# Output projection of token tiles in pairs by seven block products for eight

## The chip, the cores and the metric

The kernel runs on one core of one Trainium2 chip. Five engines work on it side by side: TensorE (PE) does matrix products into PSUM, VectorE (DVE), ScalarE (ACT) and GpSimd (POOL) do elementwise work, and SyncE (SP) issues the transfers (DMA). POOL works on SBUF tiles alone in this kernel. Each engine takes its instructions in order and waits on semaphores of the others. The metric is the device time of one execution in microseconds, the median of several runs.

## The reference

Everything is float32. `x` has 4 batches of 1024 tokens of 1024 features; there are 32 heads of 32 features.

```python
def attn(x, wq, wk, wv, wo):
    q, k, v = (x @ wq), (x @ wk), (x @ wv)          # each reshaped to (b, s, 32 heads, 32)
    q, k = rotary(q), rotary(k)
    scores = einsum('bqhd,bkhd->bhqk', q, k) / sqrt(32)
    probs = softmax(where(causal, scores, min))
    out = einsum('bhqk,bkhd->bqhd', probs, v).reshape(b, s, d)
    return out @ wo

def ffn(x, route_w, A, Bw):                          # 8 experts, rank 16, the best one alone
    logits = x @ route_w.T
    weight = one_hot(argmax(logits)) * max(logits)
    h = einsum('bsd,erd->bser', x, A)
    return einsum('bser,eor->bso', weight[..., None] * h, Bw)

x = x + attn(layernorm(x), wq, wk, wv, wo)
x = x + ffn(layernorm(x), route_w, A, Bw)
```

The change concerns `out @ wo` and the addition to `x` behind it.

## The kernel before

The work is cut into 32 units, one for each batch and each group of four heads (`units`; a batch has eight groups). A unit computes the scores of its heads in rounds (`score_round`, list `SLOTS`): PE fills four PSUM banks with the products of 32x32 blocks (L430), ACT copies them to SBUF (L441), POOL adds the causal mask on the diagonal (L444), DVE finds the row maxima (L462, and `both`, which joins the halves of a row, L483), ACT exponentiates (L491), and DVE transposes the probabilities in blocks of 32 (L516). Twice in a unit, at the slots "second" and "first", PE multiplies probabilities by values (`value_pieces`, L634) and DVE divides by the row sums (L654). A PSUM tile of four banks (`ps_s`) holds scores or values; four more banks (`ps`) serve everything else, one for each accumulation.

The probabilities of a unit lie in two tiles, `pr_{u}_0` and `pr_{u}_1` (tags `prob0`, `prob1`), each allocated anew for each unit. A query tile t takes a width that grows with t, and tiles stand `APART` from each other, so that between them there are places of at least 128 columns, in each of four heads, which hold nothing.

While a unit's scores, exponentials and values are computed, PE also works off a list of steps, `between[u]`, one list for each unit, which `fill` and `do_some` hand out slot by slot in proportion to their costs. A list holds the projections of the next unit (`chain`, L337: eight products for each of q, k, v and each half of the tokens, with the rotation behind q and k on DVE and POOL, L369 to L375), and, from the second batch on, the output projection of one token tile of the batch before (`finish_steps`).

That projection takes the attention values of 128 tokens, which each unit has stored to DRAM (`scratch`), back as `at`, transposed (`fetch`, which also loads the tile's `x` as `y`), and multiplies it by `wo` in two halves of 512 columns, eight products of 128x128 by 128x512 for each half (`project`, L751). A chunk of `wo` (256 KB) is loaded for each product into one of four buffers (`load_chunk`, L708), four ahead. DVE adds each half to `y` (L757), and behind the second half comes the layer norm (`layernorm`, L178 to L189: statistics, variance and the scaling on DVE, the root on POOL). The rest of a tile is its tail, four steps that stand in the list of the next unit: `turn` (eight transposes on PE, L201, copied back by ACT and DVE), `route` (L773, routing and hidden products, with five small operations on DVE), `turn_hidden` (L802) and `adapt` (L812, the adapters' product in two halves, each added to `y` by DVE, L815), and the store to `out`, SP's, a little later. So each of the eight units of a batch finishes one tile of the batch before; the last batch's tiles follow at the end, where `wo` is kept in SBUF.

The order of all instructions comes from this planner: steps are woven evenly (`weave`), rotations are put off by costs (`postponed`), and nothing reorders them afterwards. In the seventh unit of a batch that has a successor, the chains stand in the order `ENDING` and the last one is held back for the eighth, in which the layer norms of the next batch are woven in (`change_steps`, class `Norm`, whose `homes` say in which buffer a tile of `x` is put).

The row buffers (tag `row`, 128x1024) are five; a tile of the projection uses three of them, `at`, `y` and `yn`.

Of the kernel before, what the change touches and what calls it, by code (L numbers as in the profile page):

```python
# [9 lines left out]
F32 = mybir.dt.float32  # L10
# [61 lines left out]
def tile_preln_attn_then_top1_lora(  # L72
# [163 lines left out]
    class Two:  # L236
# [5 lines left out]
        def __getitem__(self, key):  # L242
            rows, cols = key
            k, at = divmod(cols.start, HALF)
            return self.parts[k][rows, at : at + cols.stop - cols.start]

    class Norm:


# [10 lines left out]
        def load(self, *tiles):  # L260
            u = self.b * NG
            for t in tiles:
                n = self.homes.get(t)
                if not n:
                    self.x[t] = load_x(self.b, t)
                    continue
# [421 lines left out]
    def load_adapter():  # L688

        ra_all = NC * (E + ER)  # L690
        room = big.tile([P, ra_all + D + TB * D], F32, tag="prob0", name="adapter")
# [25 lines left out]
    def finish_steps(b, t, kind="stream"):  # L717
# [126 lines left out]
        for c in range(0, NC, RA):  # L844
# [8 lines left out]
            Step(turn_hidden, 0.3),  # L853
            Step(adapt, 2.0, None if last else of_bw),
        ]
        return Step(fetch, 0.0), chains, tail


    def change_steps(u, norm, project, tail, held):
# [32 lines left out]
    tail = []  # L892
    for u, (b, g) in enumerate(units):
        project, new_tail = [], []
        if b:
            fetch, (project,), new_tail = finish_steps(
                b - 1, g, "resident" if u == len(units) - 1 else "stream"
            )
            if g:
                apart = 3 if g + 1 == NG and u + 1 < len(units) else 8  # L900
                between[-1].insert(max(0, len(between[-1]) - apart), fetch)
            else:
                late_fetch[u] = fetch

        if u + 1 < len(units) and g + 1 == NG:
            last_v = between[-1]
            if b:
                norm = Norm(b + 1, {0: (2,), 2: (5,), 3: (6,)}, {3: "q", 4: "k", 6: "q"})  # L910
                load = [Step(lambda norm=norm, t=t: norm.load(t), 0.0) for t in range(2)]
                for at, step in (
                    (own["k", 0][0], load[0]),
                    (own["v", 0][0], norm.finding(0)),
                    (own["v", 0][1], load[1]),
                    (own["v", 0][2], norm.scaling(0)),
                    (own["v", 0][4], norm.finding(1)),
                    (own["v", 0][6], norm.turning(0)),
                    (own["v", 0][7], norm.scaling(1)),
                    (own["k", 1][2], norm.finding(2)),  # L920
                    (own["k", 1][3], norm.turning(1)),
                    (own["k", 1][5], norm.scaling(2)),
                ):
                    behind(last_v, at, step)
            else:

                norm = Norm(b + 1, {0: (7,)}, {5: "chunk", 6: "chunk"})
                for v, t in (*((t + 1, t) for t in range(NG - 2)), (NG - 1, NT - 1)):
                    ahead_of[v] = (
                        lambda norm=norm, t=t: norm.find(t),  # L930
                        lambda norm=norm, t=t: norm.scale(t),
                    )
                    if v < NG - 1:
                        between[t].append(Step(lambda norm=norm, t=t: norm.load(t), 0.0))
                for at, step in (
                    (own["q", 0][0], Step(lambda norm=norm: norm.load(6), 0.0)),
                    (own["q", 1][0], norm.finding(6)),
                    (own["q", 1][3], norm.scaling(6)),
                ):
                    behind(last_v, at, step)  # L940
                for t, at in enumerate((("k", 1), ("k", 1), ("k", 1), ("v", 1))):
                    behind(last_v, own[at][(1 + 3 * t) % NC], norm.turning(t))
            steps = change_steps(u + 1, norm, project, tail, held)
            norms[b + 1] = norm
        else:
            steps = []
            held = []
            if u + 1 < len(units):


                ends = g + 2 == NG and b + 1 < B
                own = {}
                for n, tb in ENDING if ends else USUAL:
                    own[n, tb] = chain(u + 1, n, tb)
                    if ends and b and (n, tb) == ("v", 1):
                        held = own[n, tb]
                    else:
                        steps += own[n, tb]
            if not steps:
                steps = list(project)  # L960
            elif b and not g:
                steps = steps[:36] + weave(steps[36:], project)
            else:
# [263 lines left out]
```

## Time and profile before

| What | Value |
|---|---|
| Median of 3 runs | 2713.38 us (2710.95 to 2716.87) |
| Span of the profiled execution | 2709.0 us, the only time of its own that the page gives |
| PE busy | 2664.0 us, 98% |
| DVE, ACT, POOL busy | 2143.4 (79%), 1723.6 (64%), 601.9 us (22%) |
| Product of 128x128 by 128x512, L751 | 736 records with chunks, 602 ns each |
| Addition of a half to `y`, DVE L757 | 690 ns |
| POOL sum of two 128x512 tiles, L375 | 1289 ns |
| ACT copy of a 128x512 bank, L365 | 579 ns |
| 256 KB of `wo`, from issue to landing | 3.8 us |
| Mean granted TensorE clock | 0.998 |

A float32 product of the program leaves two records on PE; 368 loads of `wo` stand beside 736 records. Records overlap, so the distance of their starts, not their length, says what a product costs. In the timelines the columns are start, length, engine, line, operation, output and input with shapes, the number of records, and in brackets idle time and what ended it.

### The profile page before, as it was taken

How to read it: one execution, taken by the hardware profiler on the slowest of the kernel's cores; microseconds unless marked ns; L12 is line 12 of the kernel's file. 1: busy time of each engine (PE TensorE's matmuls, PEld its weight loads, DVE VectorE, ACT ScalarE, POOL GpSimd, SP SyncE). 2: the span in 40 equal slices, each digit the busy share in tenths (PEclk: the TensorE clock that was granted, in tenths of full speed). 3: DMA queues.
4: the chain of work that ended last, by engine and by line, in shares of the span. 5: the costliest groups of instructions: out<-in, count | busy, mean ns of one | idle time of the engine just before them, and what ended most of it. 6: DMA issues, size and time to landing. Idle time of an engine off the chain costs nothing.

```text
span 2709.0 us, 84062 instructions
## 1 busy us (share of the span) xinstructions
PE 2664.0 (98%) x35108; PEld 1300.3 (48%) x35108; DVE 2143.4 (79%) x4256; ACT 1723.6 (64%) x4978; POOL 601.9 (22%) x845
## 2 busy tenths in 40 slices
PE   8999999999999999999999999999999999999998
PEld 5444444444444544545444445444544444544445
DVE  4899988887787787887777877888787777787555
ACT  2878777876666676665666666766566666666521
POOL 2222222222222222222122222222212222212000
PEclk9999999999999999999999999999999999999999
DMA  3222323226554455652555554574355555446421
GB/s 119 60 72 73 76 72 80 64 65 176 139 141 130 124 138 154 165 164 65 164 158 134 136 132 131 137 189 140 83 158 143 154 134 138 122 132 198 127 70 53
DMA packets 465900, 332.74 MB, mean 123 GB/s; under 512 B 160880, under 2 KB 382320, under 8 KB 465520
## 3 DMA queue, kind: packets, MB, share of 16 engines
q1 hardware_dynamic: 465520, 327.37, 44.3%
q8 instruction: 276, 4.52, 0.7%
q14 instruction: 104, 0.85, 0.1%
HBM read 277.01 MB, written 50.26 MB: 121 GB/s over the span
## 4 chain that ended last, share of the span: by engine, by line
PE 80%; DVE 13%; ACT 3%; DMA 1%; issue 1%; POOL 1%; SPq 1%; POOLq 0%; DVEq 0%; ACTq 0%
PE po L751 15%; PE pq L337 14%; PE pk L337 14%; PE pv L337 12%; PE s L430 11%; PE av L634 8%; DVE top L462 4%; DVE pr L516 4%; PE ph L773 2%; PE pf L812 2%; ACT pr L491 1%; DVE both L483 1%; ACT pr L441 1%; PE pt_f L201 1%; DVE st_a L178 1%
## 5 line engine op out<-in xcount | busy, mean ns | idle before, releaser
L491 ACT ACTIVATE pr<-pr,both 128x256 f32<-128x256 f32 (+15 forms) x2048 | 1044.4, 518 | 53.6 <-DVE both L483 53.6
L441 ACT COPY pr<-s 128x640 f32<-128x640 f32 (+14 forms) x544 | 525.2, 1017 | 660.2 <-PE s L430 659.6
L462 DVE TENSOR_REDUCE top<-pr 128x2 f32<-128x960 f32 (+15 forms) x768 | 650.7, 894 | 251.4 <-POOL pr L444 250.8
L516 DVE STREAM_TRANSPOSE pr<-pr 128x1024 f32<-128x1024 f32 (+11 forms) x768 | 664.7, 908 | 34.1 <-ACT pr L491 30.7
L444 POOL TENSOR_TENSOR pr<-pr,causal_sb 128x128 f32<-128x128 f32 x512 | 237.2, 470 | 1158.3 <-ACT pr L441 1149.8
L337 PE MATMUL pv<-xnT,wv 128*128 128x512 f32 x1024 | 486.3, 602 | 0.0
L337 PE MATMUL pq<-xnT,wq 128*128 128x512 f32 x1008 | 478.1, 602 | 0.2 <-ACT xnT L203 0.2
L337 PE MATMUL pk<-xnT,wk 128*128 128x512 f32 x1008 | 477.1, 602 | 0.4 <-ACT rawq L363 0.4
L430 PE MATMUL s<-kT,qT 32*32 32x256 f32 (+4 forms) x17408 | 394.0, 386 | 9.4 <-POOL pr L444 3.2
L491 ACT ACTIVATION_READ_ACCUMULATOR pr<-pr,both 128x1 f32 x2048 | 400.8, 196 | 0.0
L751 PE MATMUL po<-chunk,attn 128*128 128x512 f32 x736 | 380.0, 602 | 2.5 <-DMA chunk<-in_wo 2.5
L430 PEld LDWEIGHTS s<-kT,qT 32*32 32x32 f32 x17408 | 187.3, 103 | 267.5 <-issue 100.7
L337 PEld LDWEIGHTS pk<-xnT,wk 128*128 128x128 f32 x1008 | 181.2, 190 | 235.7 <-issue 234.5
L337 PEld LDWEIGHTS pq<-xnT,wq 128*128 128x128 f32 x1008 | 183.2, 191 | 226.8 <-issue 225.0
L337 PEld LDWEIGHTS pv<-xnT,wv 128*128 128x128 f32 x1024 | 185.6, 190 | 218.1 <-issue 216.6
L634 PE MATMUL av<-pr,vals 64*32 64x256 f32 (+3 forms) x12288 | 272.8, 319 | 4.2 <-DVE pr L516 4.1
L634 PEld LDWEIGHTS av<-pr,vals 64*32 64x32 f32 x12288 | 213.0, 106 | 112.7 <-issue 66.1
L483 DVE TENSOR_TENSOR both<-top 32x4 f32<-32x4 f32 (+3 forms) x1152 | 207.4, 180 | 23.8
L751 PEld LDWEIGHTS po<-chunk,attn 128*128 128x128 f32 x736 | 135.6, 190 | 167.2 <-issue 149.4
L654 DVE TENSOR_TENSOR at<-av,by 128x256 f32<-128x256 f32 x128 | 48.2, 418 | 107.2 <-PE av L634 60.4
L751 PE MATMUL po<-wo,attn 128*128 128x512 f32 x256 | 116.6, 596 | 0.0
L375 POOL TENSOR_TENSOR qT<-qT,swapq 128x512 f32<-128x512 f32 x64 | 82.5, 1289 | 141.4 <-DVE swapq L371 141.4
(89 smaller groups left out, 1558.4 us busy)
## 6 DMA issues: line engine op xcount, KB each, us to landing
chunk<-in_wo SPq DMA_DIRECT2D x368, 256.0 KB, 3.8
vals<-vd SPq DMA_DIRECT2D x256, 128.0 KB, 4.3
x<-in_x SPq DMA_DIRECT2D x56, 512.0 KB, 5.4
wq<-in_wq SPq DMA_DIRECT2D x32, 512.0 KB, 4.7
wk<-in_wk SPq DMA_DIRECT2D x32, 512.0 KB, 4.0
wv<-in_wv SPq DMA_DIRECT2D x32, 512.0 KB, 4.3
vd<-vT SPq DMA_DIRECT2D x128, 128.0 KB, 4.6
out_y<-x SPq DMA_DIRECT2D x32, 512.0 KB, 2.6
```

The source lines that it names most:

```text
L337: nc.tensor.matmul(at["p"], lhsT=wt[:, c, :], rhs=xnTs[b, tb][:, c, :], start=(c == 0), stop=(c == NC - 1),)
L375: nc.gpsimd.tensor_tensor(dst[:, cols], dst[:, cols], other, ALU.add)
L430: nc.tensor.matmul(sc[i * SQ : (i + 1) * SQ, h, at : at + w].rearrange("p (j k) -> p j k", k=SQ), lhsT=of_q[rows, 2 * t + half], rhs=of_k[ ...
L441: nc.scalar.copy(pr[:, :, k0 : k0 + w], sc[:, :, at : at + w])
L444: nc.gpsimd.tensor_tensor(diagonal, diagonal, causal_sb.unsqueeze(1).to_broadcast([P, HG, SQ]), ALU.add)
L462: nc.vector.tensor_reduce(top[:, k, h : h + step], places[u, t][:, h : h + step, :], AX.X, ALU.max, negate=True,)
L483: nc.vector.tensor_tensor(dst[rows], src[rows], src[other], op)
L491: nc.scalar.activation(pr[:, h, :], pr[:, h, :], AF.Exp, bias=tops[u, t][:, h : h + 1], accum_out=dens[u, t // QT][:, t % QT, h : h + 1],)
L516: nc.vector.transpose(pr, pr)
L634: nc.tensor.matmul(avs[half][h * HD : (h + 1) * HD, t0:, :], lhsT=v[rows, j, h * HD : (h + 1) * HD], rhs=rhs, start=(j == 0), stop=(j == n ...
L751: nc.tensor.matmul(st["po"], lhsT=lhsT, rhs=rhs, start=(c == start), stop=(c == stop))
L773: nc.tensor.matmul(ph, lhsT=st["ynT"][:, c, :], rhs=w[:, c - i * RA, :], start=(c == 0), stop=(c == NC - 1),)
```

## The change

For tiles 1 and 2, 3 and 4, 5 and 6 of the first three batches, two token tiles are projected together (`pair_steps`). The two tiles' attention values and `wo` are each cut into 2x2 blocks, and the product of these is built from seven block products, p1 to p7, in place of eight. A block product is four PE products of 128x128 by 128x512, so a pair takes 28 in place of 32. Some products take sums of blocks:

- Four sums of blocks of `wo` are computed once, in the lists of the first four units, by four POOL subtractions in each, and kept in DRAM (`sum_wo`, `two_wo`): 16 loads and 16 stores of 256 KB.
- Four sums of attention blocks are computed by POOL for each pair, two of them into `s1` and `s2`, two in place.
- Products that go into more than one place are collected in `u2` and `u4`: ACT copies p1 to `u2`, DVE adds p6 to it, and p5 and that to `u4`; POOL adds `u2` and `u4` to `y` four times, and DVE adds p2, p3, p7 (twice) and p4 from PSUM.

`s1`, `s2`, `u2` and `u4` lie in the unused places between probability tiles (`gap`). For that the two probability tiles become fixed ones (`probs`). The gaps also take tile 1 of `x` of the third and fourth batch (class `Gaps`), in two transfers.

A pair's products stand in two lists: 14 in the odd unit (groups 1, 3, 5) and 14 in the even one. The first tile is complete behind p3 in the even unit, and its tail stands in the same list (`late_tail`), six or seven steps behind; the second tile's tail stands in the next unit's list, as before. The normalised tile replaces the attention values in their buffer, and the `x` tiles are loaded by steps of their own.

```diff
+    class Gaps(Two):
...
+                if n == "gap":
+                    self.x[t] = Gaps([gap(4), gap(5)])
+                    for k, part in enumerate(self.x[t].parts):
+                        source = x[self.b, t * P : (t + 1) * P, k * HALF : (k + 1) * HALF]
+                        nc.sync.dma_start(part, source.rearrange("p (c k) -> p c k", k=P))
...
+    probs = [big.tile([P, HG, WIDTH[k]], F32, tag=f"prob{k}", name=f"pr_{k}") for k in range(2)]
+    def gap(n):
+        blk, t = divmod(n, 3)
+        at = t * APART[blk] + (blk * QT + t + 1) * SQ
+        return probs[blk][:, :, at : at + P]
...
-            blocks[u, blk] = big.tile([P, HG, WIDTH[blk]], F32, tag=f"prob{blk}", name=f"pr_{u}_{blk}")
+            blocks[u, blk] = probs[blk]
...
+    two_wo = dram.tile([4, D // 2, 512], F32, tag="wo_sums", name="wo_sums", bufs=1)
+    def sum_wo(c):
+        rows = {}
+        def load():
+            for k in range(4):
+                i, n = divmod(k, 2)
+                wt = big.tile([P, 512], F32, tag="chunk", name=f"ws_{k}_{c}", bufs=4)
+                at = i * D // 2 + c * P
+                nc.sync.dma_start(wt, wo[at : at + P, n * 512 : (n + 1) * 512])
+                rows[i, n] = wt
+        def first():
+            nc.gpsimd.tensor_tensor(rows[0, 0], rows[0, 1], rows[0, 0], ALU.subtract)
+            nc.gpsimd.tensor_tensor(rows[0, 1], rows[1, 1], rows[0, 1], ALU.subtract)
+        def second():
+            nc.gpsimd.tensor_tensor(rows[1, 1], rows[1, 1], rows[0, 0], ALU.subtract)
+            nc.gpsimd.tensor_tensor(rows[1, 0], rows[1, 0], rows[1, 1], ALU.subtract)
+        def store():
+            for k, at in enumerate(((0, 0), (1, 1), (0, 1), (1, 0))):
+                nc.sync.dma_start(two_wo[k, c * P : (c + 1) * P], rows[at])
+        return [Step(f, 0.0) for f in (load, first, second, store)]
+    def pair_steps(b, t, t2):
+        st, tail = finish_steps(b, t, "pair")
+        st2, tail2 = finish_steps(b, t2, "pair")
+        s1, s2, u2, u4 = (gap(k) for k in range(4))
+        def fetch():
+            for k, tk in enumerate((t, t2)):
+                at = row(f"attn_{b}_{tk}").rearrange("p (c k) -> p c k", k=P)
+                nc.sync.dma_start(
+                    at, scratch[b][:, tk * P : (tk + 1) * P].rearrange("(c p) k -> p c k", p=P)
+                )
+                a[k, 0], a[k, 1] = at[:, : NC // 2], at[:, NC // 2 :]
+                (st, st2)[k]["home"] = at
...
+        def part(product, c, k):
...
+            if c == 0:
+                bank_of[product] = bank([P, 4, P], f"p{product}_{name}")
+            po = bank_of[product]
+            nc.tensor.matmul(
+                po.rearrange("p c k -> p (c k)"),
+                lhsT=lhsT()[:, c, :],
+                rhs=take_chunk(k),
+                start=c == 0,
+                stop=c == 3,
+            )
+            load_chunk(k + 4)
+            behind_product.get((product, c), lambda po: None)(po)
+        def sums_1(po):
+            nc.gpsimd.tensor_tensor(s1, a[1, 0], a[1, 1], ALU.add)
+        def sums_2(po):
+            minus(s2, s1, a[0, 0])
+        def sums_3(po):
+            minus(a[1, 0], a[0, 0], a[1, 0])
+        def after_p1(po):
+            nc.scalar.copy(u2, po)
+            onto(0, 0, u2, nc.gpsimd)
+        def after_p2(po):
+            onto(0, 0, po, nc.vector)
+            minus(a[0, 1], a[0, 1], s2)
+        def after_p6(po):
+            nc.vector.tensor_tensor(u2, po, u2, ALU.add)
+        def after_p5(po):
+            nc.vector.tensor_tensor(u4, po, u2, ALU.add)
+            onto(0, 1, u4, nc.gpsimd)
+        def after_p3(po):
+            onto(0, 1, po, nc.vector)
+            whole(0)
+        def after_p7(po):
+            onto(1, 1, u4, nc.gpsimd)
+            onto(1, 1, po, nc.vector)
+            onto(1, 0, po, nc.vector)
+        def sums_4(po):
+            onto(1, 0, u2, nc.gpsimd)
+        def after_p4(po):
+            onto(1, 0, po, nc.vector)
+            whole(1)
...
+        for product in ("p1", "p2", "p6", "p5", "p3", "p7", "p4"):
+            for c in range(4):
...
+        if b and 0 < g < NG - 1:
+            if g % 2:
+                fetch, loads, products, pair_tails = pair_steps(b - 1, g, g + 1)
+                between[-1].insert(max(0, len(between[-1]) - 8), fetch)
+                project = [loads[0], *products[:14]]
+            else:
+                project = [*products[14:17], loads[1], *products[17:]]
+                late_tail, new_tail = pair_tails
...
-                norm = Norm(b + 1, {0: (2,), 2: (5,), 3: (6,)}, {3: "q", 4: "k", 6: "q"})
+                norm = Norm(b + 1, {0: (2,), 2: (5,), 3: (6,)}, {1: "gap", 3: "q", 4: "k", 6: "q"})
...
+            if late_tail:
+                at = steps.index(products[19])
+                for k, s in reversed(list(enumerate(late_tail))):
+                    steps.insert(min(len(steps), at + (7 if g + 2 == NG else 6) + 8 * k), s)
...
+    for c in range(4):
+        steps = between[c]
+        for at, s in zip((0.2, 0.5, 0.65, 0.85), sum_wo(c)):
+            steps.insert(int(len(steps) * at), s)
```

More of the change, by code (lines that the diff above doesn't have):

```diff
@@ L245, in __getitem__ @@
             return self.parts[k][rows, at : at + cols.stop - cols.start]
+    class Gaps(Two):
+        def __getitem__(self, key):
+            rows, cols = key
+            k, at = divmod(cols.start, HALF)
+            if cols.stop - cols.start == P:
+                return self.parts[k][rows, at // P, :]
+            return self.parts[k][rows]
     class Norm:
@@ L265, in load @@
                     self.x[t] = load_x(self.b, t)
+                    continue
+                if n == "gap":
[3 more added lines that the diff above has]
+                        nc.sync.dma_start(part, source.rearrange("p (c k) -> p c k", k=P))
                     continue
@@ L690, in load_adapter @@
         ra_all = NC * (E + ER)
-        room = big.tile([P, ra_all + D + TB * D], F32, tag="prob0", name="adapter")
+        room = probs[0].rearrange("p h n -> p (h n)")
         kept["ra"] = room[:, :ra_all].rearrange("p (c n) -> p c n", n=E + ER)
@@ L855, in finish_steps @@
         ]
+        if kind == "pair":
+            return st, tail
         return Step(fetch, 0.0), chains, tail
+    two_wo = dram.tile([4, D // 2, 512], F32, tag="wo_sums", name="wo_sums", bufs=1)
[18 more added lines that the diff above has]
+        return [Step(f, 0.0) for f in (load, first, second, store)]
@@ new lines, in pair_steps, with load, minus, four @@
+    def pair_steps(b, t, t2):
+        st, tail = finish_steps(b, t, "pair")
+        st2, tail2 = finish_steps(b, t2, "pair")
+        name = f"{b}_{t}"
+        h = [slice(k * 512, (k + 1) * 512) for k in range(2)]
+        a, bank_of = {}, {}
+        s1, s2, u2, u4 = (gap(k) for k in range(4))
[7 more added lines that the diff above has]
+                (st, st2)[k]["home"] = at
+        def load(k):
+            (st, st2)[k]["y"] = load_x(b, (t, t2)[k])
+        def minus(dst, one, other):
+            nc.gpsimd.tensor_tensor(dst, one, other, ALU.subtract)
+        def four(ap):
+            return ap.rearrange("p (c k) -> p c k", k=P)
+        def onto(k, n, term, engine):
+            y = four((st, st2)[k]["y"][:, h[n]])
+            engine.tensor_tensor(y, term, y, ALU.add)
+        def whole(k):
+            s = (st, st2)[k]
+            s["yn"] = s["home"].rearrange("p c k -> p (c k)")
+            layernorm(s["yn"], s["y"], f"f{b}_{(t, t2)[k]}")
+        def part(product, c, k):
+            lhsT = {
+                "p1": lambda: a[0, 0],
+                "p2": lambda: a[0, 1],
+                "p6": lambda: s2,
+                "p5": lambda: s1,
+                "p3": lambda: a[0, 1],
+                "p7": lambda: a[1, 0],
+                "p4": lambda: a[1, 1],
+            }[product]
+            if c == 0:
[39 more added lines that the diff above has]
+            whole(1)
+        behind_product = {
+            ("p1", 0): sums_1,
+            ("p1", 2): sums_2,
+            ("p1", 3): after_p1,
+            ("p2", 1): sums_3,
+            ("p2", 3): after_p2,
+            ("p6", 3): after_p6,
+            ("p5", 3): after_p5,
+            ("p3", 3): after_p3,
+            ("p7", 3): after_p7,
+            ("p4", 1): sums_4,
+            ("p4", 3): after_p4,
+        }
+        rhs = {
+            "p1": wo[: D // 2, h[0]],
+            "p2": wo[D // 2 :, h[0]],
+            "p3": wo[D // 2 :, h[1]],
+            "p4": two_wo[3],
+            "p5": two_wo[0],
+            "p6": two_wo[1],
+            "p7": two_wo[2],
+        }
+        steps = []
+        for product in ("p1", "p2", "p6", "p5", "p3", "p7", "p4"):
+            for c in range(4):
+                source = ([P, 512], rhs[product][c * P : (c + 1) * P])
+                steps.append(
+                    Step(lambda ks, at=(product, c): part(*at, ks[0]), 1.0, [source])
+                )
+        loads = [Step(lambda k=k: load(k), 0.0) for k in range(2)]
+        return Step(fetch, 0.0), loads, steps, (tail, tail2)
@@ L894, in tile_preln_attn_then_top1_lora @@
         project, new_tail = [], []
-        if b:
+        late_tail = []
+        if b and 0 < g < NG - 1:
[6 more added lines that the diff above has]
+                late_tail, new_tail = pair_tails
+        elif b:
             fetch, (project,), new_tail = finish_steps(
```

## The prediction

> **What bounds the kernel now.** I read the page's shares and chain first, then the windows of single units (one batch and one group of heads), then the timeline of each engine around the instructions that the change moves.
>
> ```profile
> span 2709.0 us, 84062 instructions
> ...
> PE 2664.0 (98%) x35108; PEld 1300.3 (48%) x35108; DVE 2143.4 (79%) x4256; ACT 1723.6 (64%) x4978; POOL 601.9 (22%) x845
> ...
> PE 80%; DVE 13%; ACT 3%; DMA 1%; issue 1%; POOL 1%; SPq 1%; POOLq 0%; DVEq 0%; ACTq 0%
> ```
>
> TensorE is busy 98% of the span and carries the chain. The windows (columns: stretch, its length, busy us of each engine) show where it has no gap at all:
>
> ```profile
> 255.33:319.36 64.03, 63.40 (x1025) 29.69 (x1025) 59.40 (x119) 51.51 (x152) 17.89 (x25) 1.00 0.31 76
> ...
> 827.20:908.74 81.54, 81.54 (x1086) 39.25 (x1086) 64.79 (x129) 52.48 (x153) 18.20 (x25) 1.00 0.51 137
> 908.74:990.28 81.54, 81.54 (x1086) 39.25 (x1086) 64.79 (x129) 52.48 (x153) 18.22 (x25) 1.00 0.52 137
> ```
>
> Units that carry an output projection (the second and third row) take 81.54 us each, PE busy for all of it, and repeat to 0.01 us; what hangs on a DMA would scatter. The first batch's units (first row) have PE gaps of 0.6 to 2 us. Next, PE and then ACT around the fifteenth score tile of a unit:
>
> ```profile
> 867.43 1.14 PE L430 MATMUL s<-kT,qT 32*32 32x512 f32 x32
> 868.50 0.33 PE L802 MATMUL pw<-eye_sb,wh 128*128 128x128 f32 x1
> 868.66 1.02 PE L337 MATMUL pq<-xnT,wq 128*128 128x512 f32 x2
> 869.52 1.02 PE L751 MATMUL po<-chunk,attn 128*128 128x512 f32 x2
> 870.38 1.88 PE L337 MATMUL pq<-xnT,wq 128*128 128x512 f32 x4
> ...
> 874.93 1.98 PE L337 MATMUL pq<-xnT,wq 128*128 128x512 f32 x4
> ```
> ```profile
> 875.18 1.76 ACT L441 COPY pr<-s 128x1920 f32<-128x1920 f32 x1 [1.03 <-PE s L430]
> ...
> 878.01 0.58 ACT L363 ACTIVATE rawq<-pq 128x512 f32<-128x512 f32 x1
> ```
>
> One product (two records) moves PE on by 0.86 us: po starts at 869.52, the next at 870.38. And ACT empties the query bank (L363) at 878.01 to 878.59, 3.7 us after the score round ended (874.93), behind the copy of the scores and three exponentials. Last, VectorE (DVE) behind the round with tiles 2, 1, 0 and 9, in two units, and the layer norm behind a tile's last product:
>
> ```profile
> 1106.75 1.12 PE L751 MATMUL po<-chunk,attn 128*128 128x512 f32 x2
> ```
> ```profile
> 825.81 0.69 DVE L757 TENSOR_TENSOR x<-po,x 128x512 f32<-128x512 f32 x1 [0.84 <-PE po L751]
> 826.42 1.28 DVE L178 BATCH_NORM_STATS2 st_f<-x 128x6 f32<-128x512 f32 x2
> ...
> 828.79 0.94 DVE L189 TENSOR_SCALAR yn<-x,mv_f,rstd_f 128x1024 f32<-128x1024 f32 x1 [0.67 <-POOL rstd_f L184]
> ...
> 866.39 1.76 DVE L483 TENSOR_TENSOR both<-top 32x16 f32<-32x16 f32 x4
> ...
> 1111.05 0.71 DVE L483 TENSOR_TENSOR both<-top 32x16 f32<-32x16 f32 x4
> ```
>
> The norm is done 3.9 us after its add began. The round ended at S=1106.75 (PE's next start) and DVE finished its maxima and `both` at S+5.0.
>
> **The change, part by part.**
>
> *Products removed.* Nine pairs (tiles 1-2, 3-4, 5-6 of three batches), four products each: 36 x 0.86 = **30.9 us** off PE, 1.7 us from each of 18 full units. [...]
>
> *Banks.* Seven products need seven PSUM banks per pair where there were four, out of the same four buffers, so a bank is asked for sooner after its last use. PE takes its queue in order, so all later matmuls stand behind such a wait. Two places turn tight in the instruction order. In the nine odd units the second adapter product (pf) now reuses the query bank, and between the score round of tile 14 and it stand one pq, one pk and the first pf: 3 x 0.86 = 2.6 us, where ACT needs 3.7. In the before order five products stood there. Stall 1.1 x 9 = **9.9** (bounds 0 and 1.2 each; ACT's order ahead of L363 is as before, so near the upper). In six even units pk reuses that bank behind tile 15: PE arrives 4 products and 8 transposes later (3.43+0.93=4.4 us), ACT after its copy and six exponentials at 4.7: 0.4 x 6 = **2.4** (0 to 0.8).
>
> *The first tile's norm and tail.* They move from the next unit into the same even unit, six or seven steps behind the tile's last product (p3); before, 15 us lay between the add and the transposes (825.8 to 840.8). Each unit still has one tail: its transposes, routing products, six small DVE operations, two adds, five weight loads and a store are as many, and each SP load still waits for a PE step long past. But DVE takes the add only after `both`. In six units the norm ends at S+5.0+3.9=8.9 and PE reaches the transposes at S+9.5 (ten products of 0.86 and the round of tile 15, which moves it on by 0.96): no stall, if `both` is 0.71. In two units, the seventh of the second and third batch, whose chains stand in another order, PE is there at S+6.95 (seven products and the round): 2.0 us stall each (3.1 if `both` takes 1.76), and there the transpose of the hidden layer newly waits for ACT's copy of a bank filled one product earlier, 0.85 each. **5.7** together (0 to 8). Behind it, p4's first product takes the routing bank: DVE reaches the gate about when PE does, 0 to 0.5, I take 0.2 x 7 = **1.4**.
>
> `both` is 1.76 where a POOL multiply of two SBUF tiles ran beside it (866.3 to 867.6) and 0.71 where none did. New POOL sums could fall on it: 1.05 us on the six units' path makes 0.5 us of stall there. [...] The order puts no sum beside that `both`, so I leave it out.
>
> *POOL sums and adds.* Eight per pair of 1.28 us (row L375): 72 x 1.28 = 92 us on an engine idle 78% of the time. They stand in front of some mask adds (L444), which DVE's maxima wait for. Cover: DVE idles 17 us a unit. Taken 0, bounds 0 (work is only added) and 92. A product's sums are due six steps, some 30 us, after their inputs, so PE doesn't wait for them.
>
> *DVE and ACT.* Three more DVE adds of 0.69 per pair, 2.1 us in even units with 17 us idle, and one ACT copy of 0.58: 0; without that cover 23.8 us.
>
> *Sums of wo.* Four units of the first batch get four POOL subtractions (5.1 us beside 17.9 of 64) and eight 256 KB transfers (DMA share there 0.31). The order has them behind a mask add, not in front. Taken **1.0**, bounds 0 and 20.5 (16 x 1.28). SP waits for the subtraction before storing; it was issued well before. 36 weight loads fewer later, hidden, 0. A pair's two attention tiles come in one fetch (2 x 512 KB, 4.8 us each to land) eight steps before the unit ends, where a tile and its x came before, and the two x tiles in steps of their own, each at least 15 us before its first add, against 5.4 us to land: 0, and if a fetch were late, 4.8 per pair, 43 in all, of which I take none since the fetch has the old place.
>
> *x in the gaps.* For two batches tile 1 comes in two transfers of 512 B pieces (the like of attn<-attn, 4.8 us for 512 KB beside x's 5.4) and needs no row buffer: 0, bounds -2 and +2 each. The probability buffers are now two fixed tiles; waits in the new program go by region and none is added.
>
> Sum: -30.9 + 9.9 + 2.4 + 5.7 + 1.4 + 1.0 = **-10.5 us**. The page gives the profiled execution's span, 2709.0, and nothing around it; the median, 2713.4, is 4.4 above. Span forecast 2698.5; time **2703**.
>
> **Rivals.** (1) *Waits absorbed*: ACT gets to the bank earlier, since PE's shorter rounds pull its queue forward; stalls fall to some 5 us: 2688. For: PE waits 0.4 us for L363 in the whole trace. Against: before, five products covered it, and the three that are left are 1.1 us short by the rows shown. (2) *Stalls at their upper bounds*: 10.8+4.8+8+3.5+1 = 28, so 2711, no change that can be told: under 0.2% (5.4 us) a measurement of this kernel can't say. (3) *Slower*: POOL's queue. If the new adds in front of L444 hold up maxima, exponentials and transposes until PE waits at the value products, it costs a part of 92 us; it decides from (30.9-20.4)/92 = 11% of it, and at 25% the time is 2726. For: L462 already waits 251 us for L444 and PE 4 us for L516. Against: DVE's idle time. (4) That the products aren't saved is out: the order has 476 for 512.
>
> **How the numbers follow.** The sum as worked out 0.50 (own range 2695 to 2709), rival 1 0.15, rival 2 0.15, rival 3 0.20. Range: 2686, just under rival 1, to 2722, which cuts the worse half of rival 3. Faster: 0.46 of the first and 0.15, together 0.61; same 0.04+0.15=0.19; slower 0.20.
>
> **What would show it.** Full units of about 81 us (odd: 79.8+1.1); PE waiting for ACT L379 (the old L363) nine times 1.1 us; two PE waits of 2 us for the norm; POOL near 27%. Wrong if PE's new idle time names POOL or DVE's transposes, or if odd units take 79.8.

## The result, and the profile after

The changed kernel takes 2759.36 us in the median of four runs (2755.09 to 2762.94), the kernel before 2712.16 us beside it. The ratio is 1.0176, with a 95% interval of 1.0159 to 1.0192: 47 us slower, where 10 us faster was forecast, and 37 us above the upper end of the range. The profiled execution has a span of 2758.8 us, 49.8 above that of before.

The page of the changed kernel, with its span, its busy times and its chain:

```profile
span 2758.8 us, 84018 instructions
...
PE 2662.2 (96%) x35036; PEld 1296.9 (47%) x35036; DVE 2170.3 (79%) x4285; ACT 1734.8 (63%) x4987; POOL 713.7 (26%) x933
...
PE 76%; DVE 13%; ACT 4%; DMA 3%; issue 2%; SPq 1%; POOL 1%; POOLq 0%; DVEq 0%; ACTq 0%
```

The 72 records of the 36 products are gone, and yet PE was busy only 1.8 us less. A record that runs at a lower clock is longer (two of `po` took 2.08 us at 0.50, in unit 14 below, and two of them 1.02 at full clock in the kernel before), and that hides most of what was saved (an estimate of its share stands under the clock, further down). The rest of the 49.8 us is idle time: 96.6 us in place of 45.0. In the chain, DMA went from 1% to 3%.

Where it lies is seen by units (numbered from 0; a unit is cut here at its last scaling of values on DVE; the program issues that scaling a little way into the next unit's list, so the first steps of the next list fall into the cut). Four units of the changed kernel, one of each sort, in the windows of busy time (stretch, length, then PE, PEld, DVE, ACT and POOL, the granted clock as a share of PE's full clock, the DMA share and GB/s):

```profile
217.80:285.60 67.80, 64.35 (x1023) 30.47 (x1024) 62.32 (x119) 51.24 (x151) 22.75 (x29) 0.97 0.37 103
...
706.80:787.80 81.00, 80.14 (x1076) 37.97 (x1077) 62.61 (x124) 52.79 (x153) 22.79 (x28) 1.00 0.46 128
787.80:868.20 80.40, 80.22 (x1088) 39.12 (x1089) 68.07 (x137) 53.38 (x154) 23.81 (x30) 1.00 0.49 137
...
1110.70:1215.10 104.40, 86.92 (x1121) 43.87 (x1122) 79.01 (x163) 55.42 (x153) 21.30 (x32) 0.93 0.50 146
```

The first is unit 2, of the first batch, where sums of `wo` are made: 67.8 us for 64.1, with DVE busy 62.3 us of them. The second and the third are an odd and an even unit with a pair, at 81.0 and 80.4 us for 81.54. The last is unit 14, the seventh of the second batch; the same unit before:

```profile
1099.50:1183.80 84.30, 83.61 (x1121) 42.58 (x1122) 73.19 (x153) 55.45 (x156) 18.44 (x30) 1.00 0.68 186
```

All units together, the change in length in us:

| Units | Forecast by its terms | Measured |
|---|---|---|
| 0 to 7, first batch (sums of `wo` in 0 to 3) | +1.0 | +14.1 |
| nine odd units with a pair | 9 x (-1.71 + 1.1) = -5.5 | -5.7 |
| even units 10, 12, 18, 20, 26, 28 | 6 x (-1.71 + 0.4 + 0.2) = -6.7 | -5.3 |
| units 14 and 22 (seventh of batches two and three) | 2 x (-1.71 + 2.85) = +2.3 | +20.1 and +21.6 |
| unit 30 (seventh of the last batch) | -1.5 | +3.8 |
| 8, 15, 16, 23, 24, 31 and the end | 0 | +1.2 |
| Sum | -10.4 | +49.8 |

So the fifteen regular units came out as forecast, to 1.2 us over all of them. The loss is in two places: 42 us in two units, 14 us in the first batch.

**Units 14 and 22.** PE's waits inside unit 14 (who waited for whom: us in total, times, longest):

```profile
PE po L775 <- DMA chunk<-in_wo: 4.3, 1, 4.3
PE pt_a L201 <- DVE x L189: 3.4, 1, 3.4
PE pt_a L201 <- DVE pr L189: 2.4, 1, 2.4
PE pt_f L201 <- DVE attn L189: 2.3, 1, 2.3
PE ph L797 <- DMA chunk<-in_ra: 2.2, 1, 2.2
```

Of these only the fourth was in the forecast, with 2.0 us. Two are waits for chunks of weights. The queue of SyncE shows why they came late. SyncE's timeline after, in that unit (start, length of issuing, line, transfer, number):

```profile
1160.94 0.43 SPq L756 DMA_DIRECT2D attn<-attn  x1
1188.40 0.33 SPq L126 DMA_DIRECT2D x<-in_x  x1
1188.78 0.90 SPq L732 DMA_DIRECT2D chunk<-in_wo  x2
...
1190.90 0.70 SPq L294 DMA_DIRECT2D qT<-in_x  x1
```

and before:

```profile
1146.45 0.43 SPq L732 DMA_DIRECT2D attn<-attn  x1
1150.24 0.33 SPq L126 DMA_DIRECT2D x<-in_x  x1
```

Behind the attention values of tile 7 stands the load of that tile's `x` (its `y`). Before, it was issued 3.8 us after them; now 27.5 us after, and SyncE issued nothing in between. SyncE's waits in that stretch:

```profile
SPq L126 <- DVE x L189: 17.9, 1, 17.9
SPq L126 <- PE pt_a L201: 9.1, 1, 9.1
```

It waits for the scaling and then the transposes of a tile of the next batch's `x`, since it needs that tile's row buffer. In the kernel before, the program has this load wait for the transposes of tile 1 of that `x`; in the changed kernel tile 1 lies in the gaps and two more rows hold the pair, and the load waits for those of tile 2. Two chunks of `wo`, the next `wq`, the store of tile 5 and two tiles of `x` (L294, and DVE idles 12.4 us for the first) stand behind it.

PE's two waits for chunks cost more than their 6.5 us. The granted clock (the figure behind POOL's count) from the first of them on, and the product that came first:

```profile
1191.73:1198.56 6.83, 5.05 (x6) 1.85 (x6) 0.00 (x0) 1.81 (x8) 0.00 (x0) 0.50 0.94 329
1198.56:1201.97 3.41, 1.16 (x8) 0.91 (x8) 2.91 (x6) 1.22 (x6) 1.18 (x3) 1.00 1.07 371
1201.97:1205.39 3.42, 3.32 (x27) 2.43 (x33) 3.31 (x9) 0.00 (x0) 1.23 (x3) 0.50 1.11 331
```
```profile
1193.51 2.08 PE L775 MATMUL po<-chunk,attn 128*128 128x512 f32 x2 [4.28 <-DMA chunk<-in_wo]
```

After the gap of 4.28 us the clock is at half, and the next starts are 1.87 and 1.71 us apart where they are 0.86 elsewhere. From 1198.56 it is full, behind the second wait (2.25 us, up to 1201.09) at half again, and full from 1205.39. It was at 0.50 from 1164.43 to 1167.84 too, behind a gap of only 2.4 us, so a wait need not be as long as the 4.28 us to cost this.

**The first batch.** DVE and POOL in unit 1, where a pair of subtractions, with a product of the rotation behind it (L386), falls beside the sums of the denominators:

```profile
171.43 2.90 DVE L591 TENSOR_TENSOR rec_sb<-den 32x16 f32<-32x16 f32 x4
```
```profile
170.01 1.27 POOL L906 TENSOR_TENSOR ws<-ws,ws 128x512 f32<-128x512 f32 x1
171.36 1.28 POOL L907 TENSOR_TENSOR ws<-ws,ws 128x512 f32<-128x512 f32 x1
172.60 1.27 POOL L386 TENSOR_TENSOR kT<-rawk,cos_sb 128x512 f32<-128x512 f32 x1
```

The same four sums before took

```profile
169.73 0.80 DVE L567 TENSOR_TENSOR rec_sb<-den 32x16 f32<-32x16 f32 x4
```

The reciprocals, and with them `recs` and `by` (the transfers that carry them to the scaling of values), come later, DVE waits for `by`, and PE for the scaled values (2.1 us at 183).

### The profile page after: what moved, and what is told of

The parts are those of the page before. It is cut to its first block, busy times and chain, and to the rows that moved or that the text cites. A ratio compares the mean times of both kernels' runs of the same rounds, so it can differ in the third digit from the quotient of the medians.

```text
span 2758.8 us, 84018 instructions
## 1 busy us (share of the span) xinstructions
PE 2662.2 (96%) x35036; PEld 1296.9 (47%) x35036; DVE 2170.3 (79%) x4285; ACT 1734.8 (63%) x4987; POOL 713.7 (26%) x933
## 4 chain that ended last, share of the span: by engine, by line
PE 76%; DVE 13%; ACT 4%; DMA 3%; issue 2%; SPq 1%; POOL 1%; POOLq 0%; DVEq 0%; ACTq 0%
PE pq L353 13%; PE pk L353 13%; PE pv L353 12%; PE s L454 11%; PE av L658 8%; PE pp L966 7%; PE po L775 6%; DVE pr L540 3%; DVE top L486 3%; PE ph L797 2%; ACT pr L515 2%; PE pf L836 1%; DVE both L507 1%; ACT pr L465 1%; PE pt_f L201 1%
## 5 line engine op out<-in xcount | busy, mean ns | idle before, releaser
L353 PE MATMUL pv<-xnT,wv 128*128 128x512 f32 x1024 | 493.2, 609 | 0.0
L353 PE MATMUL pk<-xnT,wk 128*128 128x512 f32 x1008 | 488.1, 606 | 1.4 <-ACT rawq L379 1.4
L966 PE MATMUL pp<-chunk,attn 128*128 128x512 f32 x360 | 187.2, 602 | 0.0
L391 POOL TENSOR_TENSOR kT<-kT,swapk 128x512 f32<-128x512 f32 x64 | 82.0, 1281 | 121.8 <-DVE swapk L387 121.7
L386 POOL TENSOR_TENSOR kT<-rawk,cos_sb 128x512 f32<-128x512 f32 x64 | 82.0, 1282 | 119.8 <-ACT rawk L381 119.8
```

The costliest lines, as they stand in the source:

```text
L353: nc.tensor.matmul(at["p"], lhsT=wt[:, c, :], rhs=xnTs[b, tb][:, c, :], start=(c == 0), stop=(c == NC - 1),)
L386: nc.gpsimd.tensor_tensor(dst[:, cols], raw, cos_sb[:, cols], ALU.mult)
L966: nc.tensor.matmul(po.rearrange("p c k -> p (c k)"), lhsT=lhsT()[:, c, :], rhs=take_chunk(k), start=c == 0, stop=c == 3,)
```

## The experiments

The kernel before was timed again beside each group of runs, at 2711 to 2712 us; what two kernels differ by is the difference of their medians.

**The load of y later.** In the lists of the eighth units of batches two and three, at their start and so inside the cuts of units 14 and 22, `y` of tile 7 is loaded by a step of its own behind the transposes of tile 2:

```diff
-            st["y"] = load_x(b, t, homes.get(t, "row"))
+            if not y_later:
+                st["y"] = load_x(b, t, homes.get(t, "row"))
+        def fetch_y():
+            st["y"] = load_x(b, t)
...
-            ... turning(2), h[6], p[2], h[7]]
+            ... turning(2), load_y, h[6], p[2], h[7]]
```

> One edit: the last tile's x of a batch (y of tile 7) is loaded behind the transposes of tile 2 of the next x, not with its attention values, in the second and third batch's seventh unit. Theory Q (SyncE's queue): in these two units SyncE stands 27 us in front of that load, which waits for a row buffer, and two wo chunks, the next wq, an out store and two x tiles stand behind it; so the two DMA waits of PE (4.3 and 2.3 us) and the lower clock that follows them (0.93 over the unit) go, some 11 us in each, and the time is about 2737. Rival N (the norms): PE's stalls there come from DVE, which does the late tail's norm beside the next batch's norms; the load only follows that, and the time stays within 3 us of 2759.

Measured: 2732.88 us, ratio to before 1.0082 (1.0067 to 1.0096): 26.5 us under the changed kernel. Units 14 and 22 take 93.8 us each, 10.6 and 12.6 less:

```profile
1109.60:1203.40 93.80, 82.52 (x1120) 42.29 (x1121) 79.03 (x162) 55.40 (x153) 21.36 (x32) 0.98 0.56 165
```

The wait for a chunk of `wo` is gone and that for `in_ra` fell to 0.5 us, the granted clock is 0.98 in place of 0.93, PE's busy time fell by 4.4 us for as good as the same records (1120 for 1121), and the waits for the norms are as they were. Theory Q holds, and rival N is left with what remains, 9.5 and 9.1 us in these units.

**Two pairs a batch.** Tiles 5 and 6 singly, tile 1 of the next `x` in a row:

```diff
-        if b and 0 < g < NG - 1:
+        if b and 0 < g < NG - 3:
...
-                norm = Norm(b + 1, {...}, {1: "gap", 3: "q", 4: "k", 6: "q"})
+                norm = Norm(b + 1, {...}, {3: "q", 4: "k", 6: "q"})
```

> Tiles 5 and 6 are projected singly again, as before, and tile 1 of the next x has its row buffer back; the pairs 1-2 and 3-4 stay. Theory Q: the seventh units go back from 104.4, 106.4 and 93.2 to 84.3, 84.8 and 89.4 us, and the three units ahead of them lose their 0.5: 2759 - 45 + 2 = 2716. Rival C (a pair is dear wherever it stands, through POOL's additions and the clock): a third of the pairs takes a third of the loss outside the first batch away, (47 - 14)/3 = 11 us: 2748.

Measured: 2719.22 us, ratio 1.0033 (1.0021 to 1.0045). Units 14, 22 and 30 take 84.4, 84.6 and 89.4 us, as before the change, and the pairs that stay keep 81.04 and 80.4. A pair isn't dear wherever it stands.

**The sums of wo, by themselves and without the subtractions.** The first run is the kernel before with `two_wo`, `sum_wo` and the loop that places its steps, and nothing that uses them. The second leaves its two subtracting steps empty, so only transfers are added:

```diff
-        return [Step(f, 0.0) for f in (load, first, second, store)]
+        return [Step(f, 0.0) for f in (load, lambda: None, lambda: None, store)]
```

> The kernel before with the sums of wo added in their places (loads, subtractions and stores of the first four units), and nothing that uses them. Theory Q: the first units cost 14 us by themselves, without any pair: 2726. Rival: the sums cost only the 1 us of the forecast, and the longer first units come from the fixed probability buffers: 2713 to 2715.

> The kernel before with the loads and stores of the wo sums in the first four units, but without the subtractions (so what is stored are plain blocks of wo, which nothing uses). The sums as a whole cost 10.9 us. Theory Q (transfers in front of recs and by): the loads and stores cost most of it, and the time stays at 2720 or above. Theory V (POOL beside DVE): the subtractions lengthen DVE's instructions with two SBUF operands beside them (DVE's busy time in these units went from 59.4 to 62 us each, in units of 64 us), and without them the time is 2714 to 2717.

Measured: 2722.85 us, ratio 1.0043 (1.0030 to 1.0057), so the sums cost 10.9 us without any pair; and 2713.59 us, ratio 1.0009 (1.0000 to 1.0018), so the transfers cost 2 us and the subtractions the other 8 to 9. The busy times of the two runs, the one with the subtractions first:

```profile
PE 2669.3 (98%) x35108; PEld 1302.3 (48%) x35108; DVE 2152.9 (79%) x4256; ACT 1726.7 (63%) x4978; POOL 624.6 (23%) x861
```
```profile
PE 2666.1 (98%) x35108; PEld 1305.1 (48%) x35108; DVE 2143.4 (79%) x4256; ACT 1722.9 (64%) x4978; POOL 602.6 (22%) x845
```

With the same 4256 instructions DVE is busy 9.5 us longer beside the 16 subtractions, and just as long as before without them. That is theory V, though the price isn't only DVE's longer instructions. What it says of two SBUF operands shows in the trace of the changed kernel: beside a subtraction ten DVE instructions with two SBUF inputs took 4.0 us longer in all, nineteen with one 0.1 us (more of this in the last section). In units 1 to 3 DVE waits 7.9 us for `by` with the sums, and PE then 8.3 us for the scaled values; before, neither waits at all. DVE's wait for POOL's masks did not grow there: 9.2 us before, 4.9 with the sums, 6.0 in the changed kernel. With the transfers alone `by` is late too (5.3 us), yet PE loses 0.9 us. No run has the subtractions without the transfers, so how the 10.9 us split is known in this order alone.

**Other places for the sums.** In the first four units, away from the denominators:

```diff
-        for at, s in zip((0.2, 0.5, 0.65, 0.85), sum_wo(c)):
+        for at, s in zip((0.3, 0.4, 0.72, 0.82), sum_wo(c)):
```

> One edit: in the first four units the steps of the wo sums stand at 0.30, 0.40, 0.72 and 0.82 of the list instead of 0.20, 0.50, 0.65 and 0.85. Theory Q: the loads of 1 MB stand in SyncE's queue between the transfers recs and by of the reciprocals, and a pair of subtractions beside the four sums of the denominators on DVE (2.9 us for 0.8), so by comes late, and PE waits for the scaled values; away from there, about 10 of the 14 us that these units lost come back: 2749. Rival P (POOL's work as such): the subtractions stand in front of mask additions wherever they are, and the time stays at 2757 or above.

Measured: 2754.72 us, ratio 1.0159 (1.0141 to 1.0178): 4.6 us won of the 10 expected. Units 0 to 3 are 7.6 us longer than before in place of 13.6. The four sums of the denominators are back at 0.80 us; in unit 1 one subtraction now falls beside `both`, 1.65 us where it was 0.96, and `by` takes 3.1 us to issue. The collision had moved, and rival P was partly right: in units 1 to 3 DVE now waits 17.0 us for POOL's masks, 9.2 before and 6.0 in the changed kernel. The intervals of this run and of the changed kernel overlap, so the 4.6 us are not clear of the noise.

**The bank of the adapter's second product.** With the later load of `y`, and in the odd units of a pair the two adapter products four steps later:

```diff
-                steps.insert(6 + k * n // 7, s)
+                steps.insert(6 + k * n // 7 + (4 if k == 3 and b and g % 2 and 0 < g < NG - 1 else 0), s)
```

> The kernel with the later load of y (2733), and in the odd units with a pair the two adapter products of the tail stand four steps later, so that the second one no longer takes the query bank 2.6 us behind the last query product. Theory B (the bank costs what PE waits there): 9 x 0.86 us less, 2725, odd units at 80.2 us. Rival: the wait moves on to the next product that takes the bank, and the time stays at 2731 to 2735.

Measured: 2729.16 us, ratio 1.0068 (1.0055 to 1.0080), 3.7 us under the run without this; the two intervals overlap, so the medians alone don't show a gain. The odd units go from 81.04 to 80.7 us. The wait of 0.87 us for the query bank is gone; a wait of 0.5 us stands before the next product of the pair, and the profile names no cause for it. So 0.33 us of 0.86 was won in each. The rest came back at a later product, as the rival said; that it is again a bank isn't shown.

**The next norms earlier in units 14 and 22.** With both edits, tiles 0 and 1 of the next `x` loaded, found and scaled earlier, the late tail three products later, and POOL's addition of `u4` issued behind p7's first product:

```diff
-                    (own["k", 0][0], load[0]),
-                    (own["v", 0][0], norm.finding(0)),
-                    (own["v", 0][1], load[1]),
-                    (own["v", 0][2], norm.scaling(0)),
-                    (own["v", 0][4], norm.finding(1)),
-                    (own["v", 0][7], norm.scaling(1)),
+                    (own["q", 1][2], load[0]),
+                    (own["k", 0][4], norm.finding(0)),
+                    (own["k", 0][6], load[1]),
+                    (own["k", 0][7], norm.scaling(0)),
+                    (own["v", 0][1], norm.finding(1)),
+                    (own["v", 0][4], norm.scaling(1)),
```

> As with the later adapter products (2725 expected), and in the seventh units of the second and third batch the next batch's tiles 0 and 1 of x are loaded and scaled earlier, the first tile's late tail stands three products later, and POOL's addition of u4 is issued behind p7's first product, not behind its last. Theory O (order): PE's waits for the norms there (2.3, 3.4 and 2.4 us) are waits for work that DVE got too late in its own order; they go, 8 us in each of the two units: 2709. Theory D (DVE is the bound of this unit, with 79 us busy in 94): the waits come back at a later place, and no more than 3 us in each is won: 2719 or above.

Measured: 2733.83 us, ratio 1.0090 (1.0074 to 1.0105), nothing won. All three waits that it aimed at are gone from PE, and in unit 14 these stand in their place:

```profile
PE pp L972 <- DMA chunk<-wo_sums: 4.4, 1, 4.4
PE pt_f L201 <- DVE x L843: 3.0, 1, 3.0
PE ph L801 <- DVE attn L207: 2.6, 1, 2.6
```

The 4.4 us is SyncE's queue again: `recs` waited 13 us for DVE's reciprocals, with three chunks behind it. The unit takes 95.7 us. Theory D is the nearer one.

**No additions on POOL.** With the later load of `y`, POOL's additions of `u2` and `u4` to `y` are left out:

```diff
         def onto(k, n, term, engine):
+            if engine is nc.gpsimd:
+                return
```

> The kernel with the later load of y, and POOL's four additions of u2 and u4 to y of each pair left out (36 x 1.29 us of POOL; the collected products are then missing from the output, the sums of attention blocks stay). What is told apart is what still makes the seventh units of the second and third batch 9 us longer than before. Theory O (the first tile's norm and tail in front of the next norms in DVE's order): these units stay at 92 us or above, regular pair units do not move, the time is 2728 to 2733. Rival P (POOL's additions hold up DVE's, 1.9 us in front of p7's): these units fall to 90 or less, and if POOL's additions cost something everywhere the regular units fall too: 2722 or below.

Measured: 2727.59 us, ratio 1.0060 (1.0047 to 1.0073), 5 us under the run that has them. Odd and even units stay at 81.04 and 80.4 us, units 14 and 22 at 93.8. In unit 14 the wait for tile 0's norm fell from 3.4 to 0.8 us, and the next one grew:

```profile
PE pt_f L201 <- DVE x L843: 3.7, 1, 3.7
PE pt_a L201 <- DVE pr L189: 2.4, 1, 2.4
```

The wait for the transposes of tile 6 had been 2.0 us. So POOL's additions cost the pairs nothing that lasts, and theory O's number holds. The 5 us between the medians can't be placed: the profiled execution of this run has a span of 2733.8 us, above the 2729.8 of the other.

**Sums of wo in the gaps, later.** The run with the earlier norms and the sums in units 7 and 8; then a kernel with seven pairs (tiles 5 and 6 paired only where no next batch follows), adapters three steps later, and the sums in units 6 and 7:

```diff
+        paired = b and 0 < g < NG - 1 and (g < NG - 3 or b + 1 == B)
...
-                wt = big.tile([P, 512], F32, tag="chunk", name=f"ws_{k}_{c}", bufs=4)
+                wt = gap(k)
...
+    for c, (v, start) in enumerate(((6, 0.02), (6, 0.5), (7, 0.02), (7, 0.5))):
+        steps = between[v]
+        for k, s in enumerate(sum_wo(c)):
+            steps.insert(int(len(steps) * (start + 0.11 * k)), s)
```

> As with the earlier norms, and the sums of wo are made in the eighth unit of the first batch and the first unit of the second, two sets in each, in the gaps that later hold s1, s2, u2 and u4, so that they need no chunk buffer. Theory: there PE has no gap and DVE idles, so the 11 us of the first units go and little comes in their place: 10 us under the run before it, 2699 if that gives 2709. Rival: the subtractions cost PE the same wherever they stand: no gain.

> Seven pairs in place of nine: tiles 5 and 6 are paired only for the third batch, whose projection ends in no seventh unit that also norms the next batch; the tail's adapter products stand three steps later in the odd units of a pair; the sums of wo are made in the gaps in units 6 and 7 (the seventh and eighth of the first batch), two sets in each. Theory: 7 odd units at 80.7 and 7 even ones at 80.4 for 81.54, 14 us under before; the sums cost 1 us in unit 7 and some 2 in unit 6; the first unit of the second batch stays within 2 us of before: 2711 - 14 + 5 = 2702, faster than before. Rival: the wo sums or the clock take the gain back, and the time is 2709 or above.

Measured: 2729.92 us, ratio 1.0068 (1.0055 to 1.0081), for the first, 4 us under the run without the move, with overlapping intervals. Units 0 to 7 are back at the length of before (0.3 us over all eight), but unit 8, in which two sets stand among the chunks of `wo`, takes 89.2 us for 77.7: PE waits 2.9 and 2.5 us for chunks. And 2706.21 us, ratio **0.9983 (0.9973 to 0.9992)**, for the second: faster than before, by 5 us, which is less than the 0.2% that the forecast took for measurable, but its interval leaves 1 out. It lies between the theory's 2702 and the rival's 2709. Unit 8 is at 78.6 us, the pairs at 80.6 and 80.4, units 14 and 22 at 84.4. But units 5 and 6 are 2.9 and 5.9 us longer (their cuts hold the first steps of the lists of units 6 and 7). Unit 6:

```profile
477.50:553.60 76.10, 69.99 (x1071) 35.60 (x1072) 61.41 (x117) 58.02 (x163) 23.70 (x31) 0.92 0.41 100
```

PE waits 4.1 us there for the scaled values, and the clock is 0.92 over the unit.

**All four sets in unit 7, with seven and with nine pairs.**

```diff
-    for c, (v, start) in enumerate(((6, 0.02), (6, 0.5), (7, 0.02), (7, 0.5))):
+    for c, (v, start) in enumerate(((7, 0.02), (7, 0.26), (7, 0.5), (7, 0.74))):
...
-            steps.insert(int(len(steps) * (start + 0.11 * k)), s)
+            steps.insert(int(len(steps) * (start + 0.06 * k)), s)
```

> The seven pairs with one change: all four sets of wo sums stand in unit 7 (the eighth of the first batch), at 0.02, 0.26, 0.50 and 0.74 of its list with 0.06 between the steps, none in unit 6. With two sets in each, unit 5 and 6 were 2.9 and 5.9 us longer and unit 7 1.0. Theory: PE has no gap in unit 7 and DVE idles there, so unit 7 takes 2 to 3 us more than before and units 5 and 6 go back: 2706 - 8 + 1 = 2699. Rival: four sets fill POOL and the queue of unit 7, PE waits there, and the time is 2704 or above.

> All nine pairs, with the later load of y, the adapter products three steps later and the sums of wo in unit 7 as in the run beside it. Theory O (a pair in the seventh units of the second and third batch costs about 9 us there by its norm and tail, whatever else is mended): 17 us above the seven pairs, 2716. Rival: with the rest mended these units recover too, and nine pairs are as fast as seven or faster: 2700 or below.

Measured: 2710.98 us, ratio 0.9999 (0.9990 to 1.0007), a miss: unit 7 is 7.6 us longer and unit 6 still 4.3; DVE is busy 64.7 us in unit 7 where it was 58.6, and PE waits 4.5 us for scaled values there. The rival was right. And 2725.50 us, ratio 1.0054 (1.0040 to 1.0068), for nine pairs: 14.5 us above the seven, 17 expected. Units 14 and 22 take 95.2 and 95.8 us there.

## Why the prediction was wrong

- *What bounds the kernel, and the products removed.* Right. PE had no slack in the regular units: over units 9 and 10 the distances between the starts of the projection's products fell by 3.5 us, 3.4 forecast. That transfers scatter is in the trace of before: chunks of weights landed 2.1 to 8.6 us after their issue, 3.7 in the median, where the regular units repeat to 0.01 us.
- *Banks.* Right. PE waited for ACT's copy of the query nine times, 0.86 us each, 7.8 us where 9.9 was taken, and for pk in even units eight times, 1.4 us in all where 2.4 was taken. That the regular units still came out as forecast is partly luck: in units 9 and 10 PE idles 1.0 us where the terms have 1.7, but the distances between its other starts grew by 0.8 us, which no term has.
- *The first tile's norm and tail.* The waits named are there: 2.3 us for the norm in units 14 and 22 (2.0 taken) and 0.7 for ACT's copy (0.85 taken). What was not seen is what is late next. In that unit DVE also norms the next batch, and with the late tail it has 79 us of work where it had 73, while PE needs 82.5. So PE waits again at later transposes (3.4, 2.4 and 2.1 us). With the later load of `y`, which takes the queue out, these units are still 9.5 and 9.1 us longer, where the terms made 1.1 each. The run with the earlier norms and the one without POOL's additions show that such a wait moves on when one cause of it is taken away. The cover of "17 us" of DVE's idle time was read from a regular unit and did not hold in this one.
- *p4's wait for the gate*, 1.4 us: not there.
- *x in the gaps: 0, bounds -2 and +2*, and in the step before it the fetch at 0. This is the step that failed most. I priced the two transfers into the gaps and asked whether a wait was added on the gaps. I did not ask which row buffer the loads behind them would get. The load of `y` of tile 7 got the row of tile 2, whose transposes start 23 us behind those of tile 1 on PE (1187.3 and 1164.7), where it had had the row of tile 1. In the tail's step I had written that each SyncE load "still waits for a PE step long past"; for this one it was a step still to come, with everything behind it held. The later load of `y` gives back 26.5 us, 23 of them in these two units, against the 0 (at worst 2 each) of this step.
- *Sums of wo*, 1.0 us with bounds 0 and 20.5: 10.9 us by itself, 14 in the profile of the changed kernel. The order, which has the subtractions behind a mask addition, was read rightly. The term was mis-sized because the cost is not a delay of the masks: DVE's instructions take longer beside the subtractions (the same 4256 were busy 9.5 us more in the run with the sums alone), DVE had been busy 92% of these units without them (59.5 of 64.5 us in unit 1), and so the scaled values come late for PE. I had the price of such a collision, 1.05 us on `both`, and weighed it only where the pairs' sums stood.
- *POOL sums and adds of the pairs, DVE and ACT*: right at 0 in the regular units. *Rival 3* put its slower case on these additions; without the four that go to `y` the pairs' units are as long as with them. The subtractions in the first batch cost 8.5 of their 20.5 us, far above the 11% at which that rival decides, but by DVE's lengthened work and not by the masks.
- *Unit 30*: 3.8 us longer where 1.5 shorter was forecast. In the profile the store of tile 5 waits in SyncE's queue ahead of the 16 loads of the kept `wo`, and PE then waits 2.3 us (put down to DVE's `both`) and 0.9 us (to a load of `wo`). In other runs with this same order the unit was 0.1 us longer or shorter than before, and unit 31 then 1.7 us longer. The store wasn't moved by itself, so this is left open.
- The clock was in no term. It is read above; the mean granted clock, 0.989 where it was 0.998, puts an upper end of 0.009 x 2759 = 25 us on its share. PE was busy 56.4 us at half clock, 10.2 before; at full clock this work would take half as long (by the starts in unit 14, 0.86 us apart for 1.87 and 1.71), so an estimate of the share is (56.4 - 10.2) / 2 = 23 us. In units 14 and 22 the later load took 4.4 and 6.6 us off PE's busy time.

## What to carry to other kernels

A load in SyncE's queue had two prices here: its own, and that of everything behind it while it waited for its buffer (27 us in unit 14; 26.5 us of the kernel's time came back when two such loads were issued later). When buffers are moved, list for each later load which earlier use frees the buffer that it gets now, and compare the place of that use with that of the load; a load freed by a step still to come belongs behind that step. And an engine's spare time has to be read in the very unit where the work is put: here DVE had 17 us of it in a regular unit and 11 in the seventh, where after the change it had 79.0 us of work beside PE's 82.5.

## What was not expected of the hardware

In unit 14 the gap of 4.28 us on PE was followed by 5.05 us of work at a granted clock of 0.50, and the one of 2.25 us by another 3.32 us. At full clock this work would take half as long (by the same starts), 4.2 us less, so by this estimate waits of 6.5 us cost about 11 with their after-effect; the later load of `y` gave back 10.6 there.

The length of a gap alone doesn't decide. In the changed kernel the stretches at half clock last 3.41 or 6.83 us (one runs past the end of the span), and they begin whole multiples of 3.41 us apart. Cut into such pieces of 3.41 us, and without its start and end, the kernel has twelve in which PE idled 2.1 us or more, and a piece at half clock followed each; of eleven with 1.5 to 1.9 us, it followed three. The gap of 3.35 us in unit 14 fell into two pieces, with 1.61 and 1.74 us, and the clock stayed full; the gap of 2.41 us had 2.18 us in one.

Four small DVE sums of 0.80 us took 2.90 beside a POOL subtraction of 1.28 us and a POOL product of 1.27, which were not lengthened (1.28 is the mean of either kind); they ended 0.46 us behind POOL's second.

Beside the sixteen subtractions of the changed kernel DVE ran ten of these small instructions with two SBUF inputs (two halves of `den` in four sums `rec_sb`, of `top` in six `both`). Together they took 4.0 us longer than the mean of their like with no POOL instruction beside them; the nineteen row maxima and block transposes there, with one input each, 0.1 us. In the whole trace DVE's product of two SBUF tiles in the rotation (L387, 128x512) took 0.69 us in the 87 cases without a POOL instruction beside it and 1.10 in the mean of the other 41; the addition of a PSUM bank to `y` (L946) took 0.68 in either case. In the run with the sums alone, 20.5 us of subtractions added 9.5 us to DVE's busy time; which of its instructions took them was not read there.
